# A hand-ordered attention and FFN kernel: a weight split moved ahead of a norm, two norms measured one unit sooner

## The chip, the cores and the metric

The kernel runs on one core of one Trainium2 chip. The metric is the device time of one execution in microseconds (us), as a median of several runs. Five engines work side by side: PE (TensorE, matmuls; its weight loads are a second row, PEld), DVE (VectorE), ACT (ScalarE), POOL (GpSimd) and SP (SyncE, which here only issues DMAs). Each has its own instruction queue.

## The reference, cut to what matters

Four sequences of 512 rows and 512 columns go through a norm, a gated slot attention of 16 heads with a residual, a second norm, and a gated FFN with a residual.

```python
def layernorm(x): return (x - mean(x)) / sqrt(var(x) + 1e-5)
h = layernorm(x)
q, k, s = h @ Wq, h @ Wk, clip(h @ Ws, -32, 32)      # 16 heads of 64
v, g = h @ Wv, h @ Wg                                # 16 heads of 128
o = slot_attention(q, k, v, s)                       # two running sums over the rows, softmax between
o = o * rsqrt(mean(o * o) + 1e-5) * g_norm_weight
x = x + (o * silu(g)) @ Wo
h = layernorm(x)
x = x + fp8(down_w).T @ (silu(h @ fp8(gate_w) * gate_scale) * (h @ fp8(up_w) * up_scale)) * down_scale
```

The FFN's weights are rounded to eight-bit floats and used as wide ones.

## The kernel before

**Units.** The work on the attention is cut into 32 units `(g, b)`: g is a pair of heads (0 to 7), b a sequence (0 to 3). The order (line 950) is all g for the sequences 0 and 1 in turn, then all g for 2 and 3. So unit 0 is (0, 0), unit 14 is (7, 0), unit 15 is (7, 1), unit 16 is (0, 2), unit 30 is (7, 2) and unit 31 is (7, 3). A unit is one call of `attention` (line 763): it projects s, k, q, for even g also v for this and the next g, computes the slot scores and their softmax, projects g in two halves (`gate_main`, `gate_mixed`), and reads out. Output steps of the unit before (`turn_output`, `project_output`) are woven in. After the units comes the FFN (line 1001).

**Split operands.** Matmuls run on weights and activations cut into a high part and two more parts, made on the chip. `load_matrix` (line 222) splits a weight: `high` is one ACT instruction for 512 columns (line 238), `rest` two DVE instructions (lines 244 or 246, and 249). s, k and q take one such piece for each g, g takes two, v four. In the first half of the units the parts are also stored to memory (`split_`), from where the second half loads them again.

**The norm.** `layernorm(b, which)` (line 285) handles four blocks of 128 rows. `measure` is three DVE instructions and a power on POOL (lines 302 to 305), `normalise` one DVE instruction (309), `transposes` four PE transposes into a PSUM bank and one ACT copy (316, 321 or 323), `parts` two DVE instructions and one on ACT (332, 334, 337; the second norm only 332). The norm of sequence 0 comes first of all. That of sequence 1 is made in unit 0, of sequence 2 in unit 15, of sequence 3 in unit 16, and the second norm of sequence 0 in unit 31.

**The order is written by hand.** All engines run in the order in which the program emits instructions (`manual_schedule`, line 936). Small pieces of later work wait in one list, `work`; `other(n)` (line 169) emits the next n of them, with n left out as many as `pace` says. `need(key)` (line 174) emits pieces until none of that name is left. `layernorm` inserts its measures and first two normalisations into `work` behind the last piece named `xs_0` or `v` (line 353), and puts four `step`s into a second list, `steps`. `next_step()` emits one of them: whatever measure and normalisation it needs, then the transposes of one block; its `parts` go to the front of `work`. When the bank of a block is asked for again before its `parts` were emitted, `bank` (line 111) emits them first through `held`.

In unit 0, `work` begins with four `parts` of sequence 0, then the pieces of v, the norm of sequence 1, and the pieces of g, s, k and q. Projections of unit 0 emit fixed numbers of pieces ahead of ACT's eviction of the result (line 483): 4 in s, 2 in k, 1 in q. `need("g")` (line 834) stands ahead of the first gate projection. Rounding of FFN weights (`quantize`, line 391) goes through `work` too, three pieces for each of 36 slices, in the units of the sequences 2 and 3: 3 slices in an even unit and 2 in an odd one.

`pace` is 2 in a unit that has pieces of a norm in `work` (line 982), else 1, and the two `other()` ahead of `attention` go by it.

The functions named, with the line numbers of the profile:

Of the kernel before, what the change touches and what calls it, by code (L numbers as in the profile page):

```python
# [38 lines left out]
F32R = mybir.dt.float32r  # L39
# [10 lines left out]
def kernel(  # L50
# [233 lines left out]

    def layernorm(b, which, n_bank=None):

        src = x1[b]
        dst = [
            xpool.tile([P, KC, T], F32R, tag=f"xs{i}", name=f"xs{which}_{b}_{i}")
            for i in range(4 - which)  # L290
        ]
        xs[b] = dst
        start = (b, which) == (0, 1)
        if start:
            whole.append(two.tile([P, KC, T], F32, tag="v", name="xn_whole"))
        stats = two.tile([P, NT, 6], F32, tag="stats", name=f"stats{which}_{b}")
        mv = two.tile([P, NT, 2], F32, tag="mv", name=f"mv{which}_{b}")
        rstd = two.tile([P, NT], F32, tag="rstd", name=f"rstd{which}_{b}")
        xn, pts = {}, {}

        def measure(n):
            nc.vector.bn_stats(stats[:, n, :], src[:, n, :])
            nc.vector.bn_aggr(mv[:, n, :], stats[:, n, :])
            nc.vector.tensor_scalar_add(rstd[:, n : n + 1], mv[:, n, 1:2], EPS)
            nc.gpsimd.tensor_tensor(rstd[:, n : n + 1], rstd[:, n : n + 1], mhalf[:, n : n + 1], ALU.pow)

        def normalise(n):
            xn[n] = two.tile([P, D], F32, tag="xn", name=f"xn{which}_{b}_{n}")
            nc.vector.tensor_scalar(
                xn[n], src[:, n, :], mv[:, n, 0:1], rstd[:, n : n + 1], ALU.subtract, ALU.mult  # L310
            )

        def transposes(n):
            pt = bank(f"ps_xn{which}_{b}_{n}", n_bank).rearrange("p (c t) -> p c t", c=KC)
            for c in range(KC):
                nc.tensor.transpose(pt[:, c, :], xn[n][:, c * P : (c + 1) * P], ident)
            hi = dst[0][:, :, n * P : (n + 1) * P]
            if start:
                nc.scalar.copy(whole[0][:, :, n * P : (n + 1) * P], pt)
            if which == 1:  # L320
                nc.scalar.mul(hi, pt, UNDER)
            else:
                nc.scalar.copy(hi, pt)
            pts[n] = pt

        def parts(n):
            cols = slice(n * P, (n + 1) * P)
            hi, lo = dst[0][:, :, cols].bitcast(F32), dst[1][:, :, cols]
            src = pts[n]
            if start:  # L330
                src = whole[0][:, :, cols]
            nc.vector.tensor_tensor(lo, src, hi, ALU.subtract)
            if which == 1:
                nc.vector.scalar_tensor_tensor(
                    dst[2][:, :, cols], lo.bitcast(F32), -1.0 / DELTA, hi, ALU.mult, ALU.add
                )
                nc.scalar.mul(lo, lo.bitcast(F32), 1.0 / DELTA)

        if start:
            for n in range(NT):  # L340
                measure(n)
                if n > 0:
                    normalise(n - 1)
                    transposes(n - 1)
            normalise(NT - 1)
            transposes(NT - 1)
            work.extend((f"xs_{b}", lambda n=n: parts(n)) for n in range(NT))
            return
        key = f"xn{which}_{b}_"
        todo = [(key + "m", lambda n=n: measure(n)) for n in range(NT)]  # L350
        todo.insert(2, (key + "0", lambda: normalise(0)))
        todo.insert(4, (key + "1", lambda: normalise(1)))
        at = max([i + 1 for i, (name, _) in enumerate(work) if name in ("xs_0", "v")], default=0)
        work[at:at] = todo

        def step(n):
            need(key + "m")
            need(key + str(n))
            transposes(n)
            run = once(lambda: parts(n))  # L360
            held[(turn[0] - 1) % 3 if n_bank is None else n_bank] = run
            work.insert(0, (f"xs_{b}", run))
            if n + 2 < NT:
                work.insert(1, (key + str(n + 2), lambda: normalise(n + 2)))

        steps.extend(lambda n=n: step(n) for n in range(NT))


    BIG = 3.0e38
# [105 lines left out]
    def project(nm, b, name, to, between=None):  # L475
        if name == f"{nm}_0_0":
            p = ps3.tile([P, T], F32, tag="proj", name=f"ps_{name}")
            for c in range(KC):
                nc.tensor.matmul(
                    p, raw[nm, 0][0][:, c * P : (c + 1) * P], whole[0][:, c, :],  # L480
                    start=(c == 0), stop=(c == KC - 1),
                )
            other({"s": NT, "k": 2, "q": 1}[nm])
            nc.scalar.mul(to, p, QSCALE if nm == "q" else 1.0)
            if between:
                between()
            return
        p = Projection(nm, b, 0, name)
        p.main(to)
        if between:  # L490
            between()
        p.mixed()
# [270 lines left out]
    def attention(g, b, before, load):  # L763


        X = Heads(g, b)
        even = g % 2 == 0

        def output(n):
            if before:  # L770
                before.project_output(n)

        if b or g:
            need(f"xs_{b}")
            need("s")
        X.slots()
        load("s")
        if before:
            before.scale_output()
        if b or g:  # L780
            need("k")

        def running_sum():
            if before:
                before.scale_other()
            X.running_sum()
            other()

        X.keys(running_sum)
        load("k")  # L790
        if b or g:
            need("q")
        X.queries(None)
        load("q")
        X.turn_e()
        if even:
            X.turn_k()
            need(f"xs_{b}")
            need("v")
            X.values(0)  # L800
            if before:
                before.turn_output(0)
            X.key_states()
            X.inverse()
            X.values(1)
            other()
            if before:
                before.turn_output(1)
            X.query_key()
            X.values(2)  # L810
            other()
            next_step()
            X.values(3)
            load("v")
        else:
            if before:
                before.turn_output(0)
            X.turn_k()
            if before:
                before.turn_output(1)  # L820
            X.key_states()
            X.inverse()
            X.query_key()
            output(0)
            other()
            next_step()
            output(1)
        other()
        X.slot_scores()
        next_step()  # L830
        X.value_states()
        other()
        next_step()
        need("g")
        X.gate_main(0)
        X.softmax()
        X.gate_mixed(0)
        other()
        X.gate_silu(0)
        output(0 if even else 2)  # L840
        next_step()
        X.gate_main(1)
        X.slot_weights()
        X.softmax_sum()
        X.gate_mixed(1)
        load("g")
        X.gate_silu(1)
        exp_and_log()
        if even:
            output(1)  # L850
            other()
            output(2)
        X.weight_slot()
        output(3)
        load("o")
        other()
        next_step()
        X.read_out()
        return X
# [76 lines left out]
    with tc.manual_schedule(engines=EVERY):  # L936
# [16 lines left out]
        for i, (g, b) in enumerate(units):  # L953
# [13 lines left out]
                    load_matrix(nm, n // 2 if nm == "v" else n, after < len(units) // 2)  # L967

            if i == 0 or (g, b) == (0, 2):
                layernorm(b + 1, 1)  # L970
            elif (g, b) == (NG - 1, 1):
                layernorm(2, 1)
            elif last:
                layernorm(0, 2)
            if (g, b) == (0, 2):
                assert not to_fetch
                stage()
            if b > 1:
                for _ in range(min(0 if units[i] == (0, 2) else 2 if g % 2 else 3, to_come[0])):
                    work += [("round", f) for f in quantize()]  # L980
                    to_come[0] -= 1
            pace[0] = 2 if any(name.startswith("xn") for name, _ in work) else 1
            if before:
                other()
                other()
            before = attention(g, b, before, load)
            while steps:
                next_step()
# [13 lines left out]
        for b in range(B):  # L1002
            need(f"xs_{b}")
            for c in range(NFC):
# [5 lines left out]
                if b == 0 and 2 < c < 3 + NT:  # L1010
                    before.project_output(c - 3)
                if c == 1 and b + 1 < B:
                    layernorm(b + 1, 2, 2)
                if prev is not None:
                    pb, pc, parts = prev
                    if pc == 0:
# [55 lines left out]
```

## Time and profile before

| what | value |
|---|---|
| median of 3 runs | 1533.15 us (1532.83 to 1533.4) |
| profiled execution, own time | 1533.37 us |
| its span | 1531.7 us |
| mean granted PE clock | 0.996 |
| busy: PE, PEld | 1495.3 us (98%), 1130.3 us (74%) |
| busy: DVE, ACT, POOL | 1013.5, 557.7, 77.5 us |

Times are counted from the start of the span. A row of groups names the line, the engine, what is written from what, the number of instructions and the mean of one. Ends of matmuls are modelled, so that a busy PE may hold short waits. Units are told apart by the first matmul of `ps_s`: unit 0 begins at 13.0 us, unit 1 at 65.59, unit 14 at 563.03, unit 15 at 595.30, unit 16 at 633.44, unit 17 at 680.72, unit 30 at 1175.87 and unit 31 at 1208.14; the first FFN matmul (`ps_fg`) begins at 1247.74. Odd units without a norm last 32.27 to 32.33 us, and 33.04 or 33.05 in units 2, 6 and 10; even ones 43.05 to 43.09.

### The profile page before, as it was taken

To read this page: it belongs to the slowest core of one execution; us is meant where nothing else is said; L and a number is where in the kernel's file an instruction comes from. 1 tells how busy PE (TensorE), PEld (TensorE's weight loads), DVE (VectorE), ACT (ScalarE), POOL (GpSimd) and SP (SyncE) were. 2 spreads that over 40 slices of the span, in tenths; PEclk is the share of its full clock that TensorE was granted. 3 is DMA by queue.
4 is the path that set the end of the run, shared out by engine and by line. 5 is a ranking of instruction groups with operands and counts; after the bars stand their busy time and mean duration, and the time that the engine had idled before them with its cause. 6 is when DMAs were issued, how large, how long until landed. Compare 5 with 4: busy or idle time off the path is not lost.

```text
span 1531.7 us, 21585 instructions
## 1 busy us (share of the span) xinstructions
PE 1495.3 (98%) x8821; PEld 1130.3 (74%) x8821; DVE 1013.5 (66%) x1814; ACT 557.7 (36%) x942; POOL 77.5 (5%) x77
## 2 busy tenths in 40 slices
PE   7899999999999999999999999999999999999998
PEld 4677777777777776677777777777777667888886
DVE  6777747774777577776877787778777854435333
ACT  4534333433444343442433243333333332222221
POOL 1000000000000001100000000000000100000000
PEclk9999999999999999999999999999999999999999
DMA  7233303330333052115232522343234220000000
GB/s 289 103 110 152 138 15 111 152 138 14 112 150 138 15 207 76 49 42 206 71 116 81 187 91 96 105 164 116 70 117 158 90 110 1 28 0 28 1 28 28
DMA packets 59842, 149.51 MB, mean 98 GB/s; under 512 B 3848, under 2 KB 32544, under 8 KB 56672
## 3 DMA queue, kind: packets, MB, share of 16 engines
q1 hardware_dynamic: 59280, 147.34, 26.4%
q8 instruction: 69, 1.13, 0.3%
q10 hardware_dynamic: 288, 0.52, 0.1%
q14 instruction: 29, 0.24, 0.1%
q0 software_dynamic: 176, 0.28, 0.1%
HBM read 90.45 MB, written 57.67 MB: 97 GB/s over the span
## 4 chain that ended last, share of the span: by engine, by line
PE 89%; DVE 6%; ACT 3%; DMA 1%; issue 1%; POOL 0%; SPq 0%; POOLq 0%; DVEq 0%; ACTq 0%
PE ps_o L750 15%; PE ps_v L501 8%; PE ps_g L458 8%; PE ps_fu L867 5%; PE ps_fg L867 5%; PE ps_ov L694 4%; PE ps_v_m L501 4%; PE ps_g_m L469 4%; PE ps_s L458 3%; PE ps_q L458 3%; PE ps_k L458 3%; PE ps_fd L911 2%; PE ps_a L528 2%; PE ps_fe L911 2%; PE ps_b L528 2%; PE ps_ok L634 2%
## 5 line engine op out<-in xcount | busy, mean ns | idle before, releaser
L750 PE MATMUL ps_o<-w_o,oT 128*128 128x512 f32 x512 | 242.2, 605 | 0.0
L750 PEld LDWEIGHTS ps_o<-w_o,oT 128*128 128x128 f32 x512 | 93.3, 190 | 85.7 <-issue 75.7
L458 PE MATMUL ps_g<-xs,w_g 128*128 128x512 f32 x512 | 146.2, 427 | 5.8 <-ACT w_g L238 5.6
L501 PE MATMUL ps_v<-w_v,xs 128*128 128x512 f32 x512 | 132.9, 401 | 0.0
L458 PEld LDWEIGHTS ps_g<-xs,w_g 128*128 128x128 f32 x512 | 94.3, 190 | 42.5 <-issue 18.2
L758 DVE TENSOR_TENSOR x<-x,ps_o 128x512 f32<-128x512 f32 x128 | 87.6, 684 | 55.1 <-PE ps_o L750 55.1
L463 ACT ACTIVATE sg<-ps_g 128x512 f32<-128x512 f32 x64 | 38.2, 597 | 219.6 <-PE ps_g L458 219.6
L709 POOL TENSOR_TENSOR rs<-rs,mhalf 128x8 f32<-128x8 f32 x32 | 55.4, 1732 | 1133.7 <-DVE rs L706 958.9
L888 DVE SCALAR_TENSOR_TENSOR h<-ps_fu,scol,act 128x512 f32<-128x512 f32 x48 | 36.0, 750 | 114.2 <-PE ps_fu L867 111.6
L510 DVE TENSOR_TENSOR v<-v,ps_v_m 128x512 f32<-128x512 f32 x64 | 44.0, 687 | 97.4 <-PE ps_v_m L501 97.3
L501 PEld LDWEIGHTS ps_v<-w_v,xs 128*128 128x128 f32 x512 | 92.3, 188 | 20.3
L509 ACT ACTIVATE v<-ps_v 128x512 f32<-128x512 f32 x64 | 38.3, 599 | 163.5 <-PE ps_v L501 163.5
L867 PE MATMUL ps_fg<-xs,wf 128*128 128x512 f32 x384 | 96.6, 393 | 0.0
L867 PE MATMUL ps_fu<-xs,wf 128*128 128x512 f32 x384 | 95.1, 390 | 1.1 <-ACT act L885 1.1
L867 PEld LDWEIGHTS ps_fu<-xs,wf 128*128 128x128 f32 x384 | 72.0, 188 | 16.7 <-ACT act L885 1.5
L867 PEld LDWEIGHTS ps_fg<-xs,wf 128*128 128x128 f32 x384 | 71.1, 188 | 14.5
L705 DVE TENSOR_REDUCE rs<-og 128x4 f32<-128x512 f32 x64 | 43.8, 686 | 56.2 <-ACT og L704 56.2
L704 ACT ACTIVATE og<-ps_ov 128x512 f32<-128x512 f32 x64 | 38.2, 597 | 117.2 <-PE ps_ov L694 116.9
L469 PE MATMUL ps_g_m<-xs,w_g 128*128 128x512 f32 x256 | 75.3, 416 | 0.0
L501 PE MATMUL ps_v_m<-w_v,xs 128*128 128x512 f32 x256 | 68.8, 391 | 0.0
L885 ACT ACTIVATE act<-ps_fg,scol 128x512 f32<-128x512 f32 x48 | 33.0, 688 | 91.0 <-PE ps_fg L867 91.0
L694 PE MATMUL ps_ov<-v,b 128*128 128x128 f32 x512 | 65.7, 281 | 0.0
(149 smaller groups left out, 2786.5 us busy)
## 6 DMA issues: line engine op xcount, KB each, us to landing
split_v<-w_v SPq DMA_DIRECT2D x4, 3072.0 KB, 10.8
split_g<-w_g SPq DMA_DIRECT2D x8, 1536.0 KB, 6.1
w_v<-split_v SPq DMA_DIRECT2D x4, 3072.0 KB, 10.9
w_g<-split_g SPq DMA_DIRECT2D x8, 1536.0 KB, 6.8
rounded<-qw SPq DMA_DIRECT2D x36, 256.0 KB, 2.0
wf<-rounded SPq DMA_DIRECT2D x12, 768.0 KB, 5.9
w_o<-in_L_attn_Wo_dram SPq DMA_DIRECT2D x16, 512.0 KB, 3.6
split_s<-w_s SPq DMA_DIRECT2D x8, 768.0 KB, 4.3
```

The source lines that it names most:

```text
L458: nc.tensor.matmul(self.p, products(self.nm, c, self.col0, i), xs[self.b][i][:, c, :], start=(i == 0 and c == 0), stop=(i == 1 and c == KC ...
L469: nc.tensor.matmul(self.m, products(self.nm, c, self.col0, 2), xs[self.b][2][:, c, :], start=(c == 0), stop=(c == KC - 1),)
L501: nc.tensor.matmul(dst, xs[b][i][:, c, n * P : (n + 1) * P], wt["v"][:, i, c * 2 * HV : (c + 1) * 2 * HV], start=(i == which[0] and c == 0 ...
L510: nc.vector.tensor_tensor(to, to, m, ALU.subtract)
L528: nc.tensor.matmul(pa[h][:, n, :], lT[rows, cols], rT[rows, cols], start=True, stop=True)
L694: nc.tensor.matmul(po[h][:, n, :], self.bb[h][:, n, :], both_v[self.b][:, n, self.v0 + h * DV : self.v0 + (h + 1) * DV], start=False, stop ...
L705: nc.vector.tensor_reduce(rs[:, h, :], self.og[:, h], AX.X, ALU.add)
L709: nc.gpsimd.tensor_tensor(rs, rs, mhalf.rearrange("p (h n) -> p h n", h=HG), ALU.pow)
L750: nc.tensor.matmul(pp, self.oT[:, h, n * P : (n + 1) * P], wo[self.g][:, h, :], start=(h == 0), stop=(h == HG - 1),)
L758: nc.vector.tensor_tensor(to, to, pp, ALU.add)
L867: nc.tensor.matmul(pp, w[:, c * P : (c + 1) * P], xs[b][k][:, c, :], start=(c == 0 and k == 0), stop=(c == KC - 1 and k == 1),)
L911: nc.tensor.matmul(sums[n], parts[k][:, n * P : (n + 1) * P], fw[c][2], start=(c == 0 and k == 0), stop=(c == NFC - 1 and k == 1),)
```

## The change

In unit 0 the place behind which the norm of sequence 1 is inserted becomes the last piece of `xs_0`, `v` or `g`, so g's three pieces come ahead of it. The projections of s, k and q now emit 6, 1 and 3 pieces. By these numbers v's last piece is emitted in k's `running_sum` and g's three pieces ahead of the eviction of q. The step behind `gate_silu(0)` is only emitted where there is a unit before, so in unit 0 the fourth block is turned in the last step of the unit, behind `weight_slot` (`b` in the profile) and ahead of `read_out`. Its `parts` are then emitted at the beginning of unit 1. The `parts` of the third block, which `need("g")` emitted ahead of the first gate projection, are emitted behind `gate_mixed(0)`.

`layernorm` returns its transposing half as a function. In units 14 and 30 it is called for sequence 2 and for the second norm of sequence 0, and the transposing half follows in units 15 and 31. So the four measures and the first two normalisations of these norms are emitted one unit sooner, one at a time. The norm of sequence 3 stays in unit 16; there two pieces, not four, come ahead of `attention`, and the other pieces come in pairs at the later places.

`pace` is 2 where there are steps. Even units of sequence 2 take 4 slices of rounding, and even units of the sequences 2 and 3 have one more place behind v's load, so that the last slice is rounded in unit 29, not 31.

```diff
-        dst = [
-            xpool.tile([P, KC, T], F32R, tag=f"xs{i}", name=f"xs{which}_{b}_{i}")
-            for i in range(4 - which)
-        ]
-        xs[b] = dst
+        dst = []
+
+        def begin():
+            dst.extend(
+                xpool.tile([P, KC, T], F32R, tag=f"xs{i}", name=f"xs{which}_{b}_{i}")
+                for i in range(4 - which)
+            )
+            xs[b] = dst
+
...
-        at = max([i + 1 for i, (name, _) in enumerate(work) if name in ("xs_0", "v")], default=0)
+        at = max([i + 1 for i, (name, _) in enumerate(work) if name in ("xs_0", "v", "g")], default=0)
...
-        steps.extend(lambda n=n: step(n) for n in range(NT))
+        def transposing():
+            begin()
+            steps.extend(lambda n=n: step(n) for n in range(NT))
+
+        return transposing
...
-            other({"s": NT, "k": 2, "q": 1}[nm])
+            other({"s": NT + 2, "k": 1, "q": 3}[nm])
...
             X.values(3)
             load("v")
+            if b > 1:
+                other(1)
...
         output(0 if even else 2)
-        next_step()
+        if before:
+            next_step()
...
             if i == 0 or (g, b) == (0, 2):
-                layernorm(b + 1, 1)
-            elif (g, b) == (NG - 1, 1):
-                layernorm(2, 1)
-            elif last:
-                layernorm(0, 2)
+                layernorm(b + 1, 1)()
+            elif (g, b) in ((NG - 1, 0), (NG - 1, 2)):
+                transposing = layernorm(*((2, 1) if b == 0 else (0, 2)))
+            elif g == NG - 1:
+                transposing()
...
-                for _ in range(min(0 if units[i] == (0, 2) else 2 if g % 2 else 3, to_come[0])):
+                for _ in range(min(0 if units[i] == (0, 2) else 2 if g % 2 else 4 if b == 2 else 3, to_come[0])):
...
-            pace[0] = 2 if any(name.startswith("xn") for name, _ in work) else 1
+            pace[0] = 2 if steps else 1
             if before:
-                other()
-                other()
+                other(1)
+                other(1)
...
-                    layernorm(b + 1, 2, 2)
+                    layernorm(b + 1, 2, 2)()
```

More of the change, by code (lines that the diff above doesn't have):

```diff
@@ L347, in layernorm @@
             work.extend((f"xs_{b}", lambda n=n: parts(n)) for n in range(NT))
-            return
+            return None
         key = f"xn{which}_{b}_"
@@ L364, in step @@
                 work.insert(1, (key + str(n + 2), lambda: normalise(n + 2)))
-        steps.extend(lambda n=n: step(n) for n in range(NT))
+        def transposing():
+            begin()
+            steps.extend(lambda n=n: step(n) for n in range(NT))
+        return transposing
     BIG = 3.0e38
```

## The prediction

> **What bounds the kernel now.** The page's first part comes first: PE is busy all but 36 us of the span. So the change can only gain what PE loses to waits, and in waiting matmuls that count as busy.
>
> ```profile
> span 1531.7 us, 21585 instructions
> PE 1495.3 (98%) x8821; PEld 1130.3 (74%) x8821; DVE 1013.5 (66%) x1814; ACT 557.7 (36%) x942; POOL 77.5 (5%) x77
> ```
>
> Second, the waits of PE alone. The columns are the total, how often, and the longest.
>
> ```profile
> PE ps_xn L316 <- DVE xn L309: 9.3, 4, 7.2
> PE ps_g L458 <- ACT w_g L238: 5.6, 1, 5.6
> PE ps_b L528 <- DVE xs L332: 5.0, 3, 1.8
> ```
>
> The first is nearly all start-up (7.2). The 5.6 is unit 0, where the gate projection waits for g's split; the three of ps_b are units 0, 15 and 31. Third, PE's timeline where a norm is measured, units 15, 16 and 31:
>
> ```profile
> 601.68 2.11 PE L458 MATMUL ps_q<-xs,w_q 128*128 128x512 f32 x8 [0.67 <-DVE eT L473]
> 606.12 0.65 PE L518 MATMUL ps_kn<-ident,kT 128*128 128x128 f32 x4 [0.55 <-DVE kT L473]
> 639.83 2.11 PE L458 MATMUL ps_q<-xs,w_q 128*128 128x512 f32 x8 [0.67 <-DVE eT L473]
> 644.27 0.66 PE L518 MATMUL ps_kn<-ident,kT 128*128 128x128 f32 x4 [0.98 <-DVE kT L473]
> 1214.53 2.11 PE L458 MATMUL ps_q<-xs,w_q 128*128 128x512 f32 x8 [0.66 <-DVE eT L473]
> 1218.97 0.66 PE L518 MATMUL ps_kn<-ident,kT 128*128 128x128 f32 x4 [0.55 <-DVE kT L473]
> ```
>
> All six wait for an eviction on DVE that stands behind the measures. Fourth, PE in stretches of 3.4 us (busy time, granted clock, DMA share, GB/s), in unit 0 and at the end of unit 31:
>
> ```profile
> 43.77:47.18 3.41, 1.23 (x16) 1.00 0.00 0
> 47.18:50.60 3.42, 0.04 (x1) 0.50 0.00 0
> 50.60:54.00 3.40, 3.40 (x8) 0.50 0.00 0
> 1238.44:1241.85 3.41, 1.89 (x18) 1.00 0.63 207
> 1241.85:1245.26 3.41, 3.41 (x6) 0.50 1.02 419
> ```
>
> Behind a stretch that PE filled a third or 55%, the clock was half. The eight gate matmuls of unit 0 took 3.70 us, in unit 1 2.12.
>
> **What the Trainium skill says.** (1) The Trainium skill, "TensorE: Matmul & The Clock Gate", section "What's actually happening": PE's clock is judged in free-running windows of 3413 ns and falls to half behind an idle one. The trace agrees on the length (3.41 and two of it), but 1.23 and 1.89 us of work in a window didn't save the clock; 2.05 in 624.04 to 627.45 did. The measurement decides: I take 1.5 us of idling in a window as enough. (2) The Trainium skill, same page, section "Architectural detail": DVE and ACT are strict queues, only PE pulls weight loads ahead. The trace agrees: at 36.50 DVE waits for ps_v_m, xn behind it begins at 37.11, and PE stands 1.40 us. (3) The Trainium skill, "ScalarE: Activation LUTs", section "What ACT_TABLE_LOAD costs": 1283 ns and a drain of about 1380. The trace shows 1.28 (57.35) and silu at 58.65, so no drain; I use 1.28.
>
> **The norms of units 15, 16 and 31.** An undisturbed odd unit reaches ps_sk 10.41 us after its start (units 14, 18, 30). Unit 15 needs 12.17, unit 31 12.18. With the measures and first normalisations gone, both begin like any odd unit: -1.76 and -1.77. Unit 16 needs 14.60 where unit 17 needs 12.43. There two measures (0.69, 0.18 and 0.15 at a pace of 1.01) stay ahead of eT's eviction: it starts at 635.15 + 2.0 = 637.2, not 639.09, and ps_q wants it at 639.0. One normalisation and one measure stay ahead of kT: the scan ends at 640.2, kT's eviction runs 641.6 to 642.3, and ps_kn wants it at 633.44 + 8.72 = 642.2. I leave 0.17: -2.0. The last pair goes behind v's second eviction (651.69), where DVE next idles 1.28 us or more.
>
> Sum of the three: 1.76 + 1.77 + 2.0 = 5.53 us.
>
> What is moved must be hidden in units 14 and 30. Unit 14 starts with g's last rest (1.38) and a measure (1.01): eT's eviction ends at 567.8, ps_q wants it at 568.6. The second measure stands behind the scan: kT is ready at 571.8, ps_kn comes at 572.2. Normalisations and measures later take slots that hold rounding in units 18 and 30 (0.76 to 1.37 us), which last 32.3 too. The four POOL powers (0.55 each) find POOL idle. Cost 0; 0.8 if this cover fails. The transposes stay in their places, and so does ps_b's wait for the fourth block in units 15 and 31 (1.70 and 1.52 us).
>
> **Rounding.** An even unit puts two pieces behind v's load: 2.1 us of DVE, 2.5 in sequence 3, for 1.37. okT ends 0.8 to 1.1 us later; ps_okn comes 4.5 us after ps_v_m, so it waits for nothing. The max behind it starts 0.45 late, and the exponentials are ready 1.8 us before ps_w wants them. Each slice's two SP DMAs (load, store) move with it: a load waits for the store of two slices before (2.0 us), and the next on SP is w_g's, 10 us later. Cost 0; at worst 0.76 to 1.13 in each of seven units.
>
> **Unit 0, the split ahead of the norm.** g's raw weights were issued at 5.18 us with 11.0 to landing, so they are there at 16.2. Up to q, ACT has v's first two pieces in its idle 1.38 us before eT, then the third, fourth and g's two (0.61 each): g's end at 25.5, q's eviction starts at 25.55 as before. DVE ends g's rests at 28.6; v's first eviction on DVE starts at 29.02. SP's raw_s, raw_k, split_v and split_g go out earlier, at no cost. At 45.0 ps_g starts at once: 5.56 of idling and 3.70 - 2.1 = 1.6 of half clock go. Then ps_b's wait (1.79) goes with the moved block. Together 9 us.
>
> What is late next: third parts, w_s, silu and evictions, one after another. From ps_okn (47.0) on:
> - DVE: max, subtract and sg's eviction to 49.8, third parts to 51.2, wT to 51.9.
> - ACT: exponential to 49.8, waits for the parts to 51.2, their third step 51.8, w_s 52.35, table 53.65, silu 54.3, sg's second eviction 54.9.
> - DVE again: sg 55.5, w_s's rests (1.4) 56.9, first mask of b 57.6. PE has done ps_b, the fourth block and ps_ov L685 by 54.3, so L694 (2.0) waits **3.3 us** and ends at 59.6.
> - ACT squares to 60.4, DVE reduces to 61.35, a copy of scales, then the fourth parts 61.45 to 62.85 and their ACT step to 63.5. Unit 1's ps_s has done four matmuls by 60.85 and waits **2.65 us** for that step.
> So ps_s_m starts at 63.5 + 1.05 = 64.55, not 67.71: -3.15 at full clock.
>
> But both waits exceed 1.5 us in one window for nearly any phase. Half clock on L694 costs 0.95 to 1.7, about 1.2; behind the second wait up to 1.7, about 0.95 (the waits are partly run through at half). -3.15 + 1.2 + 0.95 = **-1.0**; the bounds are -3.2 (no half clock) and +0.3.
>
> **Sum.** 5.53 + 1.0 = 6.5. Against the profiled execution's own 1533.37 (1531.7 and 1.7 around the span): 1526.9; the median of the runs is 0.22 lower: **1526.7 us**. The half clock at the end of unit 31 (ps_o took 3.46 for 1.98) may be gone, -1.5, or not; ps_b's wait stays, so I count 0.
>
> **Rivals.**
> - A. Unit 0 keeps its whole gain, with no new half clock: 5.53 + 3.15 = 8.7, so 1524.5; with unit 31's half clock gone too, 1523.0. For it: ps_b's 1.70 us at 626 didn't lower the clock. Against: waits of 2.65 and 3.3.
> - B. The norms' delays come back in units 14 and 30 (0.8 each behind the measures) and unit 16 keeps 1 us: 5.53 - 2.6 = 2.9, with unit 0 at 0: 1530.3. Against: rounding fills the same slots at no cost.
> - C. Slower: the clock stays half in unit 1 behind unit 0's new waits. Beyond the share above, every us of work at half costs one, so over 6.5 us of further work at half clock (four windows or more) is where it decides; the whole unit (43 us of work) would cost 43. At 8 us: 1534.7. Against: a full window ended half clock both times.
> - The change not doing what it says: the places in the two lists leave no doubt about the order, so only the cover is uncertain.
>
> **Chances.** Forecast 0.55 (1525.0 to 1528.7), A 0.29, B 0.12, C 0.04. About 0.2% (3.07 us) is what a measurement of this kernel can tell from no change. The forecast and A lie beyond it, B straddles it (0.03 beyond): faster 0.87, same 0.09, slower 0.04. The range takes in A's lower end and stops near B, which leaves under 2 in 10 outside: 1522.8 to 1530.0.
>
> **What would show it.** Right: unit 0's ps_g follows ps_xn with no wait; the six waits above are gone except some 0.2 in unit 16; units 14 and 30 last 32.3; units 15 and 31 are 1.8 shorter, unit 16 2.0; ps_ov L694 waits some 3 us for b in unit 0 and ps_s some 2.6 for xs in unit 1, each with 0.50 of clock behind it. Wrong: units 14 or 30 over 32.5, an even unit of the sequences 2 and 3 over 43.2, or no wait at L694.

## The result and the profile after

| what | before | changed |
|---|---|---|
| median, measured side by side | 1533.16 us (1532.83 to 1536.32, 6 runs) | 1527.87 us (1526.51 to 1528.02, 6 runs) |
| ratio to before, 95% interval | | 0.9961 (0.9948 to 0.9973) |
| profiled execution, own time | 1533.37 us | 1527.82 us |
| its span | 1531.7 us | 1526.1 us |

The changed kernel is 0.39% faster; 1526.7 was predicted. The profiled executions lie 5.55 us apart, and the sum of the prediction was 6.5. Helpers stand some lines lower in the changed kernel: the projections' L458 is L468, `ps_ov`'s L694 is L704, the transposes' L316 is L322, `ps_b`'s L528 is L538.

The head of the page of the changed kernel, the span and the engines' busy time:

```profile
span 1526.1 us, 21595 instructions
PE 1495.5 (98%) x8821; PEld 1131.9 (74%) x8821; DVE 1014.9 (66%) x1814; ACT 558.2 (37%) x942; POOL 78.5 (5%) x77
```

PE is busy for as long as before (1495.3), so the 5.6 us came out of its idle time. Busy time also holds what a lower clock adds: two stretches of half clock of 3.41 us went from unit 0 and one from unit 31, and three came elsewhere, two of which are shown below. The waits of PE in the changed kernel (total, how often, longest):

```profile
PE ps_xn L322 <- DVE xn L315: 9.7, 4, 7.1
PE ps_b L538 <- DVE xs L338: 3.2, 2, 1.7
PE ps_ov L704 <- DVE b L542: 3.0, 1, 3.0
...
PE ps_s L468 <- ACT xs L343: 2.4, 1, 2.4
```

The 5.6 at `ps_g` is gone, and one of the three waits of `ps_b`. Two rows are new, `ps_ov` L704 and `ps_s` L468: the two waits that the prediction put at 3.3 and 2.65 us. PE's timeline from the first gate projection of unit 0 into unit 1, in the changed kernel (start, duration, instruction, and in brackets the wait ahead of it):

```profile
45.17 2.10 PE L468 MATMUL ps_g<-xs,w_g 128*128 128x512 f32 x8
...
57.41 3.66 PE L704 MATMUL ps_ov<-v,b 128*128 128x128 f32 x16 [3.02 <-DVE b L542]
...
64.75 2.07 PE L468 MATMUL ps_s<-xs,w_s 128*128 128x512 f32 x4 [2.40 <-ACT xs L343]
66.62 1.64 PE L479 MATMUL ps_s_m<-xs,w_s 128*128 128x512 f32 x4
```

The gate projection starts at once and at full clock, 2.10 us where it took 3.70. But `ps_ov` takes 3.66 us where the same sixteen matmuls take 2.05 in any other unit, four matmuls of `ps_s` take 2.07 (1.19 just before the wait), and `ps_s_m` 1.64 (1.07). All three stand behind the new waits. PE in stretches of 3.4 us says why (length, busy time, matmul groups, granted clock, DMA share, GB/s), in the changed kernel:

```profile
54.16:57.58 3.42, 0.41 (x7) 1.00 0.00 0
57.58:60.99 3.41, 3.41 (x16) 0.50 0.77 317
60.99:64.40 3.41, 1.36 (x6) 1.00 0.36 144
64.40:67.82 3.42, 3.07 (x7) 0.50 0.49 201
```

Each stretch at 0.50 comes after one that PE filled to 12% or 40%. A third one lies at the end of unit 15 (627.6 to 631.0, behind a stretch with 1.72 us of work), and the one at the end of unit 31 is gone. Last, PE where the three norms are made, units 15, 16 and 31, the same six rows as in the prediction, from the timeline of the changed kernel:

```profile
600.69 1.98 PE L468 MATMUL ps_q<-xs,w_q 128*128 128x512 f32 x8
604.29 0.60 PE L528 MATMUL ps_kn<-ident,kT 128*128 128x128 f32 x4
638.77 1.98 PE L468 MATMUL ps_q<-xs,w_q 128*128 128x512 f32 x8
642.12 0.66 PE L528 MATMUL ps_kn<-ident,kT 128*128 128x128 f32 x4
1211.48 1.98 PE L468 MATMUL ps_q<-xs,w_q 128*128 128x512 f32 x8
1215.08 0.60 PE L528 MATMUL ps_kn<-ident,kT 128*128 128x128 f32 x4
```

None of the six has a bracket: all six waits are gone.

To see where the time went, the lengths of the units (from one unit's first `ps_s` to the next one's) are set against those of before. Unit 0 is counted from the start of the span. A unit is called even or odd by its g, so that units 14, 15, 30 and 31 (g = 7) are odd, and 0, 1 and 16 even.

| unit | changed minus before, us | what it holds |
|---|---|---|
| 0 and 1 | -0.33 | the start of g gained, two waits and two stretches of half clock |
| 14 | +0.13 | two measures and more that were moved in |
| 15 | -0.08 | its start -1.74, a stretch of half clock at its end +1.66 |
| 16 | -1.92 | |
| 31 | -3.35 | its start -1.75, the half clock at its end gone -1.6 |
| all others | within 0.1 each | |
| first FFN matmul | -5.56 | the sum |

### The profile page after: what moved, and what is told of

The parts are those of the page before. It is cut to its first block, busy times and chain, and to the rows that moved or that the text cites. A ratio compares the mean times of both kernels' runs of the same rounds, so it can differ in the third digit from the quotient of the medians.

```text
span 1526.1 us, 21595 instructions
## 1 busy us (share of the span) xinstructions
PE 1495.5 (98%) x8821; PEld 1131.9 (74%) x8821; DVE 1014.9 (66%) x1814; ACT 558.2 (37%) x942; POOL 78.5 (5%) x77
## 4 chain that ended last, share of the span: by engine, by line
PE 91%; DVE 5%; ACT 3%; issue 1%; DMA 0%; POOL 0%; ACTq 0%; DVEq 0%; POOLq 0%
PE ps_o L760 15%; PE ps_v L511 8%; PE ps_g L468 8%; PE ps_fu L880 5%; PE ps_fg L880 5%; PE ps_ov L704 4%; PE ps_v_m L511 4%; PE ps_g_m L479 4%; PE ps_s L468 3%; PE ps_k L468 3%; PE ps_q L468 3%; PE ps_fd L924 2%; PE ps_a L538 2%; PE ps_fe L924 2%; PE ps_b L538 2%; PE ps_ok L644 2%
## 5 line engine op out<-in xcount | busy, mean ns | idle before, releaser
L468 PE MATMUL ps_g<-xs,w_g 128*128 128x512 f32 x512 | 144.4, 423 | 0.3
L468 PEld LDWEIGHTS ps_g<-xs,w_g 128*128 128x128 f32 x512 | 93.3, 188 | 36.5 <-issue 18.2
L704 PE MATMUL ps_ov<-v,b 128*128 128x128 f32 x512 | 67.3, 286 | 3.0 <-DVE b L542 3.0
L468 PE MATMUL ps_s<-xs,w_s 128*128 128x512 f32 x248 | 65.8, 407 | 2.4 <-ACT xs L343 2.4
```

The source lines that it names most:

```text
L468: nc.tensor.matmul(self.p, products(self.nm, c, self.col0, i), xs[self.b][i][:, c, :], start=(i == 0 and c == 0), stop=(i == 1 and c == KC ...
L704: nc.tensor.matmul(po[h][:, n, :], self.bb[h][:, n, :], both_v[self.b][:, n, self.v0 + h * DV : self.v0 + (h + 1) * DV], start=False, stop ...
```

## The theory and its rivals

**Theory.** The norms' measures, moved a unit sooner, carry the gain (5.4 us). In unit 0 the 9 us saved are given back almost whole: by two new waits behind one chain of DVE and ACT work, and by the half clock that each of them can bring.

**Rival 1.** Unit 0 carries the gain, and the norms' delays come back elsewhere. **Rival 2.** The waits alone give unit 0's gain back, and the half clock behind them has no weight. **Rival 3.** Within unit 0 it is the block that was turned later, not the split of g, which makes the waits. **Rival 4.** Part of what was put down to the norms comes from the rounding that was moved.

Unit 0 is judged below by one measure, the stretch from its projection of k (first `ps_k`, 18.27 us in the changed kernel) to unit 1's projection of q (first `ps_q`, 70.84). The projection ahead of it falls into the kernel's first rise of the clock (16.5 to 18.7 us), so that the first `ps_k` begins at 18.25 us in one execution and at 19.29 in another, which this leaves out. The stretch is 52.92 us before and 52.57 changed.

## The experiments

All times below are medians of several runs with the kernel before beside them, each ratio being that to the kernel before, with its 95% interval. Lengths of units and stretches are read from the one profiled execution of each kernel. Where no half clock plays a part they agree closely between kernels: unit 16 is 1.87 to 1.92 us shorter than before in each kernel that has its change.

### The two halves of the change apart

The norms and the rounding alone, unit 0 as before:

```diff
-        at = max([i + 1 for i, (name, _) in enumerate(work) if name in ("xs_0", "v", "g")], default=0)
+        at = max([i + 1 for i, (name, _) in enumerate(work)
+                  if name in ("xs_0", "v") or (name == "g" and (b, which) != (1, 1))], default=0)
...
-            other({"s": NT + 2, "k": 1, "q": 3}[nm])
+            other({"s": NT, "k": 2, "q": 1}[nm])
...
-        if before:
-            next_step()
+        next_step()
```

> The changed kernel with unit 0 as it was before: the norm of sequence 1 ahead of g's pieces, the old numbers of pieces in s, k and q, the fourth block ahead of the second gate projection. Theory (the norms of units 15, 16 and 31 carry the gain, unit 0 almost none): the starts of units 15 and 31 lose 1.76 and 1.77 us, unit 16 1.9, so 5.4 us below the kernel before where the same half-clock stretches fall (1.5 us up or down for each that comes or goes): 1526.3 to 1529. Rival (unit 0 carries half of the gain or more): 1530 or above.

And unit 0 alone, the same three edits the other way round in the kernel before:

> The kernel before with the edits of unit 0 alone: g's pieces ahead of the norm, 6, 1 and 3 pieces in s, k and q, the fourth block behind b. Theory: units 0 and 1 together gain 0.2 to 1.0 us, as the wait of 5.56 us and its half clock are replaced by waits of about 3.0 and 2.4 us with half clock behind each: 1532 to 1533.2, no difference that can be told. Rival (unit 0 carries the gain): 1529 or below.

Measured: the norms alone 1530.35 us (1528.71 to 1532.75, 9 runs), ratio 0.9973 (0.9963 to 0.9983); unit 0 alone 1534.49 us (1532.39 to 1534.97, 12 runs), ratio 0.9995 (0.9987 to 1.0004). The kernel before was at 1535.14 in these runs (1531.92 to 1536.66), so by the medians the norms give 4.8 us (4.1 by the ratio) and unit 0 gives 0.65, which can't be told from nothing. Both medians lie above what was expected, 1530.35 even in the range given to its rival. Those ranges were reckoned from a kernel before at about 1533, so the differences in the same runs decide. In the profiles, the norms alone shorten unit 16 by 1.87 and unit 31 by 3.36 and have again a stretch of half clock in unit 15; units 0 and 1, which are as before there, are 1.26 longer. Unit 0 alone has the stretch from k to q at 52.40 (-0.52), with waits of 3.01 and 2.08. It has the half clock in unit 15 too (+1.65), though nothing of unit 15 was changed. Unit 0 doesn't carry the gain, so rival 1 falls.

The runs of the norms alone lie in two groups, 1528.7 to 1530.4 and 1532.5 to 1532.8, and those of the kernel before too, near 1533.1 and near 1536.2. A stretch of half clock more or less costs about 1.6 us, as units 15 and 31 show, so two of them are the size of this step. The mean granted clock of each run fits: 0.994 in the four longer runs of the norms alone and 0.995 or 0.996 in the other five, where one stretch of 3.41 us at half is 0.0011 of the span, an estimate from these figures. Where the stretches lie wasn't traced run by run.

### The clock held in the two waits

Three idle matmuls of 512 columns (six in the trace) are issued in each of the two waits; their result goes nowhere. Nothing else is changed in the changed kernel.

```diff
+    def filler(src, count):
+        whole_eT.append(src)
+        for _ in range(count):
+            nc.tensor.matmul(spare[0], tri, src, start=True, stop=True)
...
             for i in range(2):
+                if i == 1 and self.name == "s_0_1":
+                    filler(whole_eT[0], 3)
...
+            if self.u == "0_0":
+                spare.append(ps3.tile([P, T], F32, tag="proj", name="ps_spare"))
+                filler(self.eT, 3)
```

> The changed kernel with three idle matmuls of 128x512 (results not used) on PE in each of the two waits of unit 0 and 1, ahead of ps_ov on b and between the two passes of unit 1's ps_s. Nothing is left out. Theory (the 3.66 us of ps_ov and the 2.07 and 1.64 us of ps_s and its mixed part are half clock, caused by the idling): granted clock 1.00 there, ps_ov back at about 2.05 us, ps_s_m at 1.07; 2.5 to 3 us off the two units, so about 1525. Rival (the slow matmuls wait on something else, such as late operands): they stay as slow, no gain or a loss of some tenths.

Measured: 1525.49 us (1525.22 to 1526.03), ratio 0.9937 (0.9923 to 0.9952). PE's timeline of this kernel, the same place as above:

```profile
58.01 2.05 PE L717 MATMUL ps_ov<-v,b 128*128 128x128 f32 x16 [0.24 <-DVE b L552]
...
63.77 1.20 PE L478 MATMUL ps_s<-xs,w_s 128*128 128x512 f32 x4
```

`ps_ov` takes 2.05, `ps_s` 1.20 and `ps_s_m` 1.08 again. `ps_ov` begins no sooner: 3.95 us after the step ahead of the wait (54.06), where the changed kernel has 3.96. The stretch from k to q is 49.58 us, 3.34 below before and 2.99 below the changed kernel. So of what unit 0 gives back, the half clock is 3.0 us and the two bare waits are 5.4 (3.02 and 2.40); rival 2 falls.

### The fourth block turned early again

In the changed kernel, `step` behind `gate_silu(0)` is emitted in unit 0 too, as before the change. The split of g stays ahead of the norm.

```diff
         output(0 if even else 2)
-        if before:
-            next_step()
+        next_step()
```

> The changed kernel with the fourth block of unit 0 turned ahead of the second gate projection, as before; g's pieces stay ahead of the norm. Theory (moving the block traded ps_b's wait for one of ps_s on its parts): the wait of ps_s in unit 1 (2.40) and its half clock go, ps_ov's or ps_b's wait on DVE grows by about 2 us, since the block's parts and its ACT copy stand ahead of the masks of b. Units 0 and 1 together shorter by 0.5 to 1.5 us, so 1526.5 to 1527.5. Rival (moving the block is what saves unit 0 from a loss): longer by 1 us or more.

Measured: 1526.81 us (1526.44 to 1527.03), ratio 0.9946 (0.9929 to 0.9963). The stretch from k to q is 49.46 us, 3.11 less than in the changed kernel. PE's timeline of this kernel:

```profile
56.63 1.07 PE L538 MATMUL ps_b<-wT,eT 64*128 64x128 f32 x13 [3.93 <-DVE xs L338]
```

There is one wait of 3.93 in place of two of 5.42 together, and one stretch of half clock in place of two: `ps_ov` takes 2.85 us, but unit 1's `ps_s` runs its eight matmuls without a wait in 2.12 us, and `ps_s_m` takes 1.07. So of the two edits of unit 0, the split of g earlier gains 3.46 us (52.92 to 49.46), and turning the block later loses 3.11 again, more than the 0.5 to 1.5 expected. Rival 3 holds in part. The split of g makes a wait by itself: `ps_b` waits 3.93 us here and waited 1.79 before. Turning the block later adds 1.49 us of waiting and made room for a second stretch of half clock, which doesn't always come: against a second execution of the changed kernel, shown below (50.21), it loses 0.75. It is the one part of the change that these profiles show to harm; the intervals of the two ratios overlap.

### Four pieces, not two, ahead of unit 16

```diff
             if before:
-                other(1)
-                other(1)
+                other()
+                other()
```

> The changed kernel, but the two places ahead of attention go by the pace again, so that unit 16 starts with four pieces of its norm and not two. Theory (the pieces ahead of eT's eviction are the cost): ps_q and ps_kn of unit 16 wait again, 0.67 and 0.98 us, and unit 16 goes from 45.4 to about 47.3 us, all other units as in the changed kernel; 1.9 us above it. Rival (unit 16 gained from the later pieces going in pairs): unit 16 stays near 45.4.

Measured: 1528.32 us (1528.24 to 1529.4), ratio 0.9962 (0.9948 to 0.9977). PE's timeline of this kernel in unit 16:

```profile
638.16 2.11 PE L468 MATMUL ps_q<-xs,w_q 128*128 128x512 f32 x8 [0.68 <-DVE eT L483]
...
642.60 0.66 PE L528 MATMUL ps_kn<-ident,kT 128*128 128x128 f32 x4 [0.97 <-DVE kT L483]
```

The two waits of before are back (0.67 and 0.98 there), and the unit is as long as before to within 0.03 us. So it is the two pieces fewer ahead of attention that carry the 1.9 us of unit 16, wholly; the later pairs don't. The whole time is hardly above that of the changed kernel, where 1.9 was expected: the profiled execution had no half clock in unit 15 (-1.72 against -0.08), which is worth nearly as much.

### Rounding as before

```diff
-            if b > 1:
-                other(1)
...
-                for _ in range(min(0 if units[i] == (0, 2) else 2 if g % 2 else 4 if b == 2 else 3, to_come[0])):
+                for _ in range(min(0 if units[i] == (0, 2) else 2 if g % 2 else 3, to_come[0])):
```

> The changed kernel with the rounding as before: 3 slices in each even unit, no place more behind v's load. Theory (rounding is hidden on DVE both ways): no unit differs from the changed kernel by over 0.2 us apart from half-clock stretches. Rival (the last slice in unit 31 was part of its excess): unit 31 longer by 0.5 us or more.

Measured: 1526.83 us (1525.84 to 1528.93), ratio 0.9953 (0.9938 to 0.9968). Apart from the units 0, 1, 14, 15, 16 and 31 no unit differs from before by over 0.1. Unit 31, without half clock as in the changed kernel, is 2.41 shorter than before where the changed kernel is 3.35 shorter. DVE's timeline of this kernel in unit 31 and, behind it, PE's:

```profile
1213.19 0.69 DVE L425 SCALAR_TENSOR_TENSOR qw<-q 128x512 f32<-128x512 f32 x1
1213.80 0.68 DVE L483 TENSOR_TENSOR kT<-kT,ps_k_m 128x512 f32<-128x512 f32 x1
```

```profile
1214.53 0.66 PE L528 MATMUL ps_kn<-ident,kT 128*128 128x128 f32 x4 [0.74 <-DVE kT L483]
```

The last step of the last slice's rounding (L425) stands ahead of kT's eviction, and `ps_kn` waits 0.74 for it, where the changed kernel has no wait. This was not expected (0.2 at most). So rival 4 is right for unit 31: of its 1.75 us at the start, 0.94 need the rounding out of that unit as well as the measures. In the other units the move of the rounding shows in no length, neither as a cost nor as a gain.

### The changed kernel once more

The changed kernel was run again, unaltered, with another kernel beside it.

> The changed kernel again beside the kernel before and the last version on one chip. Theory: 1526 to 1528.5, in groups about 1.5 us apart as stretches of half clock come and go behind the same waits; the norms of units 15, 16 and 31 carry the difference to the kernel before. Rival (the difference of 5.3 us was a matter of the first chip's stretches alone): within 3 us of the kernel before.

Measured: 1527.5 us (1526.5 to 1527.89), ratio 0.9956 (0.9944 to 0.9969). Its profiled execution took 1526.5, 1.3 less than the first one. PE's timeline of this second execution at the end of unit 15:

```profile
624.54 1.13 PE L538 MATMUL ps_b<-wT,eT 64*128 64x128 f32 x14 [1.69 <-DVE xs L338]
625.60 1.98 PE L760 MATMUL ps_o<-w_o,oT 128*128 128x512 f32 x4
```

And of the first execution, the changed kernel above:

```profile
625.92 1.13 PE L538 MATMUL ps_b<-wT,eT 64*128 64x128 f32 x14 [1.69 <-DVE xs L338]
626.97 3.20 PE L760 MATMUL ps_o<-w_o,oT 128*128 128x512 f32 x4
```

The same kernel, the same wait of 1.69 us: once `ps_o` takes 3.20 and once 1.98. The stretch from k to q is 50.21 us here and was 52.57. `ps_ov` in unit 0 took 2.69 us behind its wait of 3.01. The half clock then reached into the first four matmuls of `ps_s` (2.01 us for 1.19), which shortened the second wait to 1.52, and no half clock followed that. Unit 15 had none and unit 31 had one. So which of the shorter waits bring half clock changes from one execution to the next.

The Trainium skill, "TensorE: Matmul & The Clock Gate", section "What's actually happening", says that the window is free-running and doesn't start with the kernel. The traces agree. In each of them all changes of the granted clock lie whole multiples of 3.413 us apart, so every execution has a fixed grid of windows, and the grid lies otherwise in the next one. Here are the windows around the two waits above, from the grid of the first execution and from that of the second:

```profile
624.19:627.60 3.41, 1.72 (x17) 1.00 0.82 252
627.60:631.01 3.41, 3.41 (x12) 0.50 0.77 291
```

```profile
622.89:626.30 3.41, 1.76 (x16) 1.00 0.78 270
626.30:629.72 3.42, 3.42 (x27) 1.00 0.73 272
```

In the first, the wait begins 0.03 us behind a boundary and lies wholly in one window; in the second it begins 0.04 us ahead of one and reaches into two. The twelve executions profiled here hold twenty such waits at `ps_b` in the units 15 and 31, of 1.52 to 1.71 us. Twelve lie wholly in one window, and half clock followed ten of them; the other two, both of 1.52, lie within 0.05 us of the window's edge. Eight lie across a boundary, and half clock followed none.

### A version that has neither wait

Two experiments follow what was learnt; the third takes both. The first writes unit 0's end anew: the third and fourth block are turned together, the masks of b are put on DVE ahead of the rests of w_s, and the two silus come together behind them. `mixed(False)` leaves its subtraction to `gate_subtract`, both in the part left out.

```diff
...
         X.gate_mixed(0)
+        if not before:
+            third = work.pop(0)
+            next_step()
+            work.insert(0, third)
+            other(1)
+            X.gate_main(1)
+            fourth = work.pop(0)
+            other(1)
+            X.slot_weights()
+            X.pg.mixed(False)
+            work.insert(0, fourth)
+            other(1)
+            X.softmax_sum()
+            X.weight_slot()
+            other(1)
+            other(1)
+            X.gate_subtract()
+            X.gate_silu(0)
+            X.gate_silu(1)
+            exp_and_log()
+            other(1)
+            other(1)
+            X.read_out()
+            return X
```

> The changed kernel with the end of unit 0 in another order: third and fourth block one behind the other ahead of the second gate projection, the masks of b ahead of w_s's rests and of the second gate subtraction, both silus together behind them. Nothing is left out. Theory (the two waits of the changed kernel are the queue order of DVE and ACT, not the work): ps_ov waits under 1 us for b, ps_s of unit 1 not at all for xs, the clock stays 1.00 in both units; ps_s_m of unit 1 starts near 59.5 us, not 66.6, so 7 to 8.5 us off: 1519 to 1521. Rival (DVE and ACT have too much work there for any order): waits of 2 us or more appear elsewhere in the two units, gain under 3 us.

Measured: 1521.8 us (1521.29 to 1522.31), ratio 0.9918 (0.9903 to 0.9933), a little less gain than expected. The stretch from k to q is 45.76, 6.81 below the changed kernel. PE's timeline of it:

```profile
55.63 2.05 PE L705 MATMUL ps_ov<-v,b 128*128 128x128 f32 x16 [0.24 <-DVE b L543]
```

`ps_ov` waits 0.24 and not 3.02, `ps_s` not at all. What is late next is eT's eviction in unit 1, for which `ps_q` waits 1.25 us; the rests of unit 1's q weights stand ahead of it on DVE.

The second turns the fourth block of units 15 and 31 ahead of the silu, and puts its `parts` behind the transposes of the slot weights:

```diff
         other()
+        early = bool(steps) and not even
+        if early:
+            next_step()
         X.gate_silu(0)
...
         X.slot_weights()
+        if early:
+            other(1)
```

> The changed kernel with the fourth block of units 15 and 31 turned ahead of silu and its parts emitted behind wT. Theory (ps_b waits there for a bank whose reader stands at the end of DVE's queue): ps_b's waits of 1.69 and 1.52 us fall to 0.6 or less, and no half clock follows them; 2.0 to 2.4 us off, and 1.3 to 1.5 more where the half clock of unit 15 goes: 1523.5 to 1525.8. Rival (the delay only moves on along DVE to the masks of b): ps_ov waits for b instead, gain under 0.7 us.

Measured: 1523.32 us (1521.62 to 1523.44), ratio 0.9925 (0.9908 to 0.9941). Unit 15 is 3.28 shorter than before and unit 31 4.73. PE's timeline of it in unit 15:

```profile
623.86 1.74 PE L538 MATMUL ps_b<-wT,eT 64*128 64x128 f32 x16
```

The wait of 1.69 at `ps_b` is gone, and with it the half clock that it could bring. The third kernel has both edits, and q's rests, which unit 0 emits for unit 1, are put ahead of its read-out:

```diff
...
+            rest = work.pop(0)
+            other(1)
             X.gate_subtract()
             X.gate_silu(0)
             X.gate_silu(1)
             exp_and_log()
+            work.insert(0, rest)
```

> The changed kernel with the new order at the end of unit 0, the fourth block of units 15 and 31 turned early, and q's rests emitted ahead of unit 0's read-out instead of unit 1's beginning. Nothing is left out. Theory (the three edits lie in different units and add up): 6.2 us of units 0 and 1 against the kernel before, 1.25 more as ps_q of unit 1 no longer waits for eT's eviction, 3.3 in unit 15, 1.9 in unit 16, 3.2 to 4.7 in unit 31: 15.9 to 17.3 us off, so 1515.5 to 1517.5. Rival (a stretch of half clock takes the place of each one removed): 1519 or above.

Measured: 1514.95 us (1514.54 to 1515.85), ratio 0.9874 (0.9859 to 0.9889), 12.6 us under the changed kernel's 1527.5 in the same runs and a little more than expected. Beyond the start-up (7.1 us) no single wait over 1.9 us is left, the longest being the 1.83 of `ps_xn` in unit 0, and no unit has a stretch of half clock. The stretch from k to q is 44.35 us. By units, as in the table above: 0 and 1 together -7.72, 14 +0.13, 15 -3.29, 16 -1.88, 31 -4.73, together -17.49 us.

## Why the prediction was right

**The norms of units 15, 16 and 31 (5.53).** Right. Measured 1.74, 1.92 and 1.75 at the places named, 5.41 us, and unit 14 took 0.13 more. The reason was right too, with one correction: in unit 31 the rounding's move carries 0.94 of it, which the working gave to the norm alone. The cover in units 14 and 30 held: they last 32.40 and 32.28 us.

**Rounding at nothing.** Right in every even unit. That it was needed in unit 31 was missed: its cost was zero, its worth wasn't.

**Unit 0 (1.0).** The mechanism was right and the sum too large: 1.0 was predicted, and the stretch from k to q is 0.35 shorter. Its terms, from the profile of the changed kernel:

| term | predicted | measured |
|---|---|---|
| `ps_g` starts | at once, 45.0 | at once, 45.17 |
| wait at `ps_ov` | 3.3 | 3.02 |
| wait at `ps_s` | 2.65 | 2.40 |
| half clock on `ps_ov` | 1.2 | 1.6 (3.66 for 2.05) |
| half clock behind the second wait | 0.95 | 1.45 (2.07 and 1.64 for 1.19 and 1.07) |
| wait of `ps_xn` for the first block | unchanged, 1.40 | 1.83 |

The gain at full clock, put at 3.15, is borne out by the kernel that held the clock (3.34). (The 67.71 of that sum is where `ps_s` ends before the change, 65.59 + 2.12, and 64.55 is such an end too, so the difference stands; the trace has `ps_s_m` begin at 67.55.) The half clock was mis-sized, 3.05 against 2.15 of the working, in this execution. The waits that were 0.5 us shorter and the 0.43 of `ps_xn` about cancel. One execution doesn't settle this term. The stretch is 52.29 to 52.64 us in five kept executions that have unit 0 as changed, and 50.21 in a sixth (the changed kernel's second, with one half clock less); in the two with unit 0 as before it is 52.92 and 53.33. So how near the total came to its figure is in part the luck of the stretches of half clock. Why `ps_xn` waits longer, 1.82 or 1.83 in every kernel with g's split ahead of the norm, stays open: in the changed kernel v's third eviction on DVE starts at 36.94 where it started at 36.50, though the matmuls that it reads start at 35.33 in both. The chain that the working laid out by hand is the one that the profile names. The changed kernel's chain of waits (start, duration, engine, what is written):

```profile
51.12 0.63 ACT xs L343
51.76 0.52 ACT w_s L238
...
52.29 1.28 ACT L744
...
54.22 0.49 ACT sg L473
...
54.73 0.69 DVE sg L483
...
56.67 0.70 DVE b L542
```

From the third block's last step on ACT (51.12) to the mask of b (56.67), nothing in this chain is b's own work: it is w_s, a table load (52.29) with the silu behind it, the second half of the gate on ACT and on DVE, and w_s's rests on DVE, all queued ahead of b. `ps_b` itself, which the mask reads, was done by 52.9. That is why another order of the same instructions could gain 6.8 us against this execution.

**Unit 31's half clock (0 counted).** It went in the first profiled execution, -1.6, and one came in unit 15, +1.66; that the two cancelled is luck. In the second both units were as before the change, so there 0 was right in each place. The prediction took 1.5 us of idling in a window as enough. The windows of the twelve executions, laid out by their grids up to 25 us ahead of the end, put this more exactly. All 14 full-clock windows with 1.40 us of PE work or less were followed by half clock, none with more than 1.90 was, and of the 18 in between (1.65 to 1.90) ten were. So 1.5 us of idling is where it begins to happen, not where it is sure. What decides between 1.65 and 1.90 stays open; the ends of matmuls are modelled, so the sums are not exact there. A wait of 1.69 us can moreover fall into two windows. The Trainium skill, "TensorE: Matmul & The Clock Gate", section "HAM oscillation — how this bites in real kernels", gives as its rule no idle gaps over some 3.4 us. The runs here differ: the bare wait of 3.0 us was followed by half clock in every execution that had it (`ps_ov` took 2.69 to 3.66 us for 2.05), and those of 1.52 and 1.69 in some. The measurement decides.

**The rivals.** A (no new half clock) is shown wrong by the two stretches at 0.50. B is wrong, since the norms' delays didn't come back and unit 16 kept 1.92. C is wrong: each half clock of the changed kernel ended after one window, and unit 1's k projection takes 2.00.

## What to carry to other kernels

In an order written by hand, a piece moved ahead isn't paid for by its own duration but by what now stands behind it on its engine: here 7.2 us of waiting and half clock were removed from one projection and 1.8 of waiting from `ps_b`, and 8.5 came back 12 to 20 us later, as waits for b and for the fourth block's parts (5.4) and as half clock behind them (3.05), though b and the parts are no more work than before. Follow the queue from the moved piece to the next instruction that PE waits for, and reorder that too; doing so was worth 6.8 us more in unit 0, half clock included. And count up to 1.7 us on top of a wait of PE of 1.5 us or more, an estimate from half of one window of 3.41 us; the largest that was measured is 1.66, and the shortest wait that had it was 1.52.

## What the runs showed that was not expected

- Matmuls whose result goes nowhere, 2.84 and 2.74 us of them in waits of 3.02 and 2.40 (the second overlaps the matmuls ahead of it in the trace), shortened the stretch by 3.0 us: filling a wait was faster than leaving it empty.
- Executions of one kernel differ by 1.3 us and more, in steps, by where the waits fall in PE's clock windows. A change of 1.5 us in one unit of one trace needs a second execution ahead of any explanation: unit 15 changed by +1.65 in a kernel in which nothing of it was altered. Its wait of 1.71 us lay in one window there, and before the change in two.
- Rounding costs nothing in the units that take it up, and was worth 0.94 us in the one that it left.
